# One head in eight: the softmax maxima added by an accumulating DMA in place of a GpSimd subtraction (LSH attention and gated feed-forward, one core)

## The chip, the cores and the metric

The kernel runs on one core of one Trainium2 chip. The metric is the device time of one launch in microseconds (us). The kernel before took 1372.26 us (median of 3 runs, 1371.28 to 1372.66).

## The reference

The input x is 16 sequences of 512 positions with 128 features, float32. Two residual blocks follow each other; the layer norms have no learned scale.

```
x = x + ln(attn(ln(x)))        # 16 heads of 8 features; queries also serve as keys
x = x + ln(ffn(ln(x)))

attn: q = x Wq^T + bq; v = x Wv^T + bv
      bucket(s,h) = 6 sign bits of [q, 1] . hyperplanes, read as a number of 0..63
      logits[s,t] = (q_s . q_t) / sqrt(128) * (62 + (bucket_s == bucket_t))
      out = softmax(logits) v
ffn:  h = silu(x w1^T s1) * (x w2^T s2); h = gelu(h h1^T s); h = gelu(h h2^T s); h w3^T s3
```

What matters here is the softmax. The matrix of logits of a head is symmetric (the coefficient is, and the keys are the queries), so the maximum of row s is also the maximum of column s. The kernel subtracts the maxima along columns, takes the exponential, and multiplies from the left with the values and a column of ones.

## The kernel before, in words

**Work.** 16 sequences of 16 heads make 256 heads, numbered j. A head's logits are a tile `l` of 128 partitions x 4 x 512 float32 (1 MB), of which there are 11 buffers (`LB`). Each head passes these steps:

- `gather` (L787): SP, the queue of the SyncE engine, issues three loads, `ql` and `qr` (72 rows of 512 bf16: the queries, split into three bf16 parts) and `bb` (the bucket numbers, the same row on all 128 partitions). Four heads can be loaded ahead.
- `scores` (L838): four TensorE (PE) matmuls `sp` into PSUM, three PSUM banks for them. `coeffs` (L855): VectorE (DVE) makes four tiles `co` of coefficients, 62 or 63, from `bb`.
- `logits` (L879): four DVE instructions multiply `co` with `sp` into `l` and leave the maximum of every row in one column of `mxpad`.
- `maxima` (L919): from head 4 on this is done for two heads together. DVE transposes `mxpad` in blocks into `mt` (128 x 32), and SP stores `mt` to DRAM as `md`, 16 KB.
- `softmax` (L933): SP loads a head's 512 maxima from `md` onto all 128 partitions (`mb`, 256 KB, three buffers); GpSimd (POOL) subtracts, `l = l - mb`, over 2048 elements a partition (L947); ScalarE (ACT) takes the exponential in place (L952).
- `attend` (L957): for each group of four heads, once all four exponentials are there, PE multiplies the values with them (`av`); ACT copies the result (`avs`), PE turns it back (`op`), DVE divides by the sums. Only then do the four `l` buffers come free.

`residual` (L1018) and `ffn` (L1041) follow per sequence. Their layer norms use POOL for one small power each (L450, 128 x 4), and the feed-forward uses PE (`w` L1088, `hp` L1122, `yp` L1156), ACT (silu L1074, gelu L1135) and DVE (`h` L1057). `inputs` (L510) prepares the input norms in three groups, with a power on POOL each (L561). Before the first feed-forward, PE fills its idle time with matmuls on zeros, `activity` (L1244).

**Order.** All steps are Python generators under a planner, the class `Order` (L47). It keeps a clock per engine; each step names its engine, a cost and a rank, and an engine that is free takes the ready step of lowest rank (ACT: the earliest, with a surcharge for a change of its function table). The order that results is written into each engine's instruction stream once and for all. On the chip every engine and each issuing queue works through its stream in that order; an instruction that waits holds up what is behind it. Three of the planner's lines matter:

```
            elif want[0] == "rest":
                self._at(self.now + want[1], self._step, p, None)
                return
```

A step `rest` makes a generator come back so many planned us later, and takes no engine; nothing of it is left in the instruction streams but the place of what follows.

Of the kernel before, what the change touches and what calls it, by code (L numbers as in the profile page):

```python
# [13 lines left out]
F32 = mybir.dt.float32  # L14
BF16 = mybir.dt.bfloat16
AF = mybir.ActivationFunctionType
ALU = mybir.AluOpType
# [4 lines left out]
P = 128  # L22
# [168 lines left out]
def tile_lsh_attention_ffn(  # L191
# [20 lines left out]
    nc = tc.nc  # L212
    B, S, E = x.shape
# [4 lines left out]
    NT = S // P  # L218
    NC = HID // P
    GH = 4  # L220
    NG = H // GH
    Q = P // GH
# [9 lines left out]
    SCALE = 1.0 / math.sqrt(E)  # L232
    AHEAD = 1
    MH = 2
    LB = 11
    SLOTS = H * NT
    N = B * SLOTS
# [3 lines left out]
    p2 = ctx.enter_context(tc.tile_pool(name="p2", bufs=2))  # L241
    ps_b = ctx.enter_context(tc.tile_pool(name="ps_b", bufs=1, space=PSUM))
    dram = ctx.enter_context(tc.tile_pool(name="dram", bufs=2, space=DRAM))

    od = Order()
# [17 lines left out]
        out=hb_sb,  # L263
        in_=hyper[DH].unsqueeze(0).unsqueeze(2).to_broadcast([H, NH, 1]),
# [73 lines left out]
    def dve(cost, rank, emit):  # L338
        return ("op", "DVE", cost, emit, rank, None)

    def act(cost, rank, emit, table=None):
        return ("op", "ACT", cost, emit, rank, table)

    def pool(cost, rank, emit):
        return ("op", "POOL", cost, emit, rank, None)

    def dma(kb, rank, emit, held=True, cost=0.35):
        return ("dma", "SP", cost, emit, rank, None, kb, held)

    def get(kind):  # L350
        return ("get", kind)
# [4 lines left out]
    def events(n):  # L356
        return [Event() for _ in range(n)]
# [4 lines left out]
    banks = Pool("b", 2)  # L362
    logit_bufs = Pool("l", LB)
    row_bufs = Pool("r", 4)
# [10 lines left out]
    gathered, exped = events(B * H), events(B * H)  # L375
# [503 lines left out]
    def logits():  # L879
        for j in range(B * H):  # L880
            kl = yield get(logit_bufs)
            if j < SINGLES or j % MH == 0:
                km, pair = (yield get(mx_bufs)), []
# [28 lines left out]
            pair.append((j, l))  # L912
            if j < SINGLES or len(pair) == MH:
                od.spawn(maxima(pair, mx, km))
# [4 lines left out]
    def maxima(heads, mx, km):  # L919


        mt = p2.tile([P, Q], F32, tag="mt", name=f"mt_{heads[0][0]}")
        yield dve(0.14, 0, lambda: nc.vector.transpose(mt, mx))
        od.put(mx_bufs, km)

        md = dram.tile([Q, GH, Q], F32, tag="md", name=f"md_{heads[0][0]}", bufs=4)
        yield dma(
            16, 0, lambda: nc.sync.dma_start(out=md.rearrange("t k q -> k t q"), in_=mt), cost=0.6
        )
        for i, (j, l) in enumerate(heads):  # L930
            od.spawn(softmax(j, l, md[i * NT : (i + 1) * NT]))

    def softmax(j, l, md):  # L933

        km = yield get(mb_bufs)
        mb = p1.tile([P, S], F32, tag=km, name=f"mb_{j}")
        yield dma(
            256,
            0,
            lambda: nc.sync.dma_start(  # L940
                out=mb, in_=md.rearrange("t k q -> (t k q)").partition_broadcast(P)
            ),
        )
        yield pool(
            4.52,
            1,
            lambda: nc.gpsimd.tensor_tensor(  # L947
                l, l, mb.unsqueeze(1).to_broadcast([P, NT, S]), op=ALU.subtract
            ),
        )  # L950
        od.put(mb_bufs, km)
        yield act(1.82, 0, lambda: nc.scalar.activation(l, l, AF.Exp, scale=SCALE), "exp")  # L952
        od.set(exped[j])
# [367 lines left out]
```

## Time and profile before

| | |
|---|---|
| time, median of 3 runs | 1372.26 us (1371.28 to 1372.66) |
| the profiled execution: its time / its span | 1373.08 us / 1371.3 us |
| granted TensorE clock, mean | 0.991 |
| first `w` matmul (the feed-forward begins) | 169.9 us |
| last logits instruction of DVE | 1263 us |
| last POOL subtraction ends | 1281.5 us |
| DMA, mean over the span | 128 GB/s |

The span runs from the first to the last instruction; 1.8 us of the execution's time lie around it. The kernel has a start of some 25 us until the first logits, a long middle in which attention of one sequence and feed-forward of earlier ones run together, and, from 1263 us, an end of 108 us in which the last two feed-forwards run alone. Shares of busy time over the whole span mix these three.

### The profile page before, as it was taken

The numbers are of one execution on the slowest core, as the hardware profiler recorded it, in microseconds if no ns is written. First come the engines' busy times: TensorE is split into PE (matmuls) and PEld (weight loads), VectorE is DVE, ScalarE is ACT, GpSimd is POOL, SyncE is SP. The second block draws the span as 40 slices with busy tenths as digits, with TensorE's granted clock in tenths as the row PEclk, the third lists the DMA queues.
The fourth block names the chain that finished last, engine by engine and source line by source line (L and its number), as shares of the span: only waits on it lengthen the run. The fifth ranks groups of instructions, "written<-read, shape, count | busy, mean of one in ns | idle before, by whom it ended". The sixth has DMA issues, their size and how long they took to land.

```text
span 1371.3 us, 21177 instructions
## 1 busy us (share of the span) xinstructions
PE 1317.3 (96%) x5922; PEld 550.9 (40%) x5922; DVE 1236.0 (90%) x3989; ACT 1127.8 (82%) x1607; POOL 1217.1 (89%) x319
## 2 busy tenths in 40 slices
PE   9999999999889999999999999999999999999996
PEld 3433334334334434343434434343434434343443
DVE  5999999999889999999999999999999999998210
ACT  2567798999779888988989888988989888988852
POOL 1599999999999999999999999999999999999400
PEclk9999999999899999999999999999999999999998
DMA  5756455445435455445545455454545454453000
GB/s 143 194 148 157 133 150 145 140 140 141 134 106 153 125 130 142 138 138 132 147 116 147 129 134 135 139 139 135 142 124 141 135 134 135 132 122 101 24 8 8
DMA packets 159837, 175.39 MB, mean 128 GB/s; under 512 B 34280, under 2 KB 117480, under 8 KB 159720
## 3 DMA queue, kind: packets, MB, share of 16 engines
q1 hardware_dynamic: 156909, 170.56, 45.4%
q10 hardware_dynamic: 2811, 3.48, 0.8%
q8 instruction: 47, 0.77, 0.2%
q14 instruction: 70, 0.57, 0.1%
HBM read 154.81 MB, written 19.17 MB: 127 GB/s over the span
## 4 chain that ended last, share of the span: by engine, by line
PE 50%; DVE 24%; POOL 9%; issue 8%; DMA 6%; ACT 2%; SPq 1%; POOLq 0%; DVEq 0%; ACTq 0%
PE hp L1122 18%; PE av L973 12%; DVE l L894 11%; PE sp L847 9%; DVE co L865 8%; POOL l L947 8%; PE w L1088 4%; PE yp L1156 3%; DMA mb<-md 3%; DMA bb<-bkd 1%; DMA qd<-q 1%; PE op L994 1%; PE vp L760 1%; POOL rs_x L561 1%; DMA qr<-qd 1%
## 5 line engine op out<-in xcount | busy, mean ns | idle before, releaser
L947 POOL TENSOR_TENSOR l<-l,mb 128x2048 f32<-128x2048 f32 x256 | 1156.1, 4552 | 43.4 <-DVE mxpad L894 24.0
L894 DVE CUSTOM_DVE_ANT_0 l<-co,sp 128x512 f32<-128x512 bf16 x1024 | 665.7, 681 | 13.8 <-PE av L973 6.9
L952 ACT ACTIVATE l<-l 128x2048 f32<-128x2048 f32 x256 | 484.6, 1907 | 40.9 <-POOL l L947 39.4
L1122 PE MATMUL hp<-h,h 128*128 128x512 f32 x1024 | 498.6, 596 | 0.3 <-ACT h L1135 0.3
L865 DVE TENSOR_SCALAR co<-bb,bj 128x516 bf16<-128x516 bf16 x1024 | 455.0, 472 | 3.3 <-DMA bb<-bkd 3.1
L847 PE MATMUL sp<-qr,ql 72*128 72x512 bf16 x1024 | 358.0, 382 | 26.7 <-DVE mxpad L894 22.5
L1122 PEld LDWEIGHTS hp<-h,h 128*128 128x128 f32 x1024 | 190.1, 190 | 185.6 <-issue 151.6
L973 PE MATMUL av<-l,vaug 128*32 128x512 f32 x2048 | 263.6, 603 | 0.0
L847 PEld LDWEIGHTS <-ql 72*128 72x128 bf16 x1024 | 94.1, 97 | 313.9 <-issue 290.7
L1088 PE MATMUL w<-xnt_f,w 128*128 128x512 f32 x256 | 132.0, 601 | 2.5 <-ACT a L1074 2.4
L952 ACT ACT_TABLE_LOAD x86 | 110.3, 1283 | 1.5
L1251 PE MATMUL activity<-still 128*128 128x512 bf16 x402 | 106.6, 385 | 1.0 <-DVE still L280 1.0
L973 PEld LDWEIGHTS av<-l,vaug 128*32 128x32 f32 x2048 | 47.4, 109 | 116.5 <-issue 93.9
L894 DVE DVE_READ_ACCUMULATOR2_ANT mxpad<- 128x1 f32 x1024 | 85.7, 84 | 0.0
L450 POOL TENSOR_TENSOR rs_y<-ve_y,mhalf 128x4 f32<-128x4 f32 x16 | 16.1, 1006 | 67.1 <-issue 34.7
L1057 DVE TENSOR_TENSOR h<-w,a 128x512 f32<-128x512 f32 x64 | 43.7, 682 | 35.2 <-PE w L1088 30.3
L1135 ACT ACT_TABLE_LOAD x58 | 74.4, 1283 | 0.9
L987 ACT COPY avs<-av 128x512 f32<-128x512 f32 x64 | 37.0, 578 | 40.0 <-PE av L973 39.9
L1088 PEld LDWEIGHTS w<-xnt_f,w 128*128 128x128 f32 x256 | 46.9, 191 | 53.1 <-issue 21.8
L1156 PEld LDWEIGHTS yp<-w,h 128*128 128x128 f32 x512 | 65.0, 196 | 7.3 <-issue 4.0
L1156 PE MATMUL yp<-w,h 128*128 128x128 f32 x512 | 66.6, 281 | 0.1
L1251 PEld LDWEIGHTS <-still 128*128 128x128 bf16 x402 | 39.1, 99 | 56.5 <-issue 19.0
(94 smaller groups left out, 941.7 us busy)
## 6 DMA issues: line engine op xcount, KB each, us to landing
mb<-md SPq DMA_DIRECT2D x256, 256.0 KB
bb<-bkd SPq DMA_DIRECT2D x256, 130.5 KB
ql<-qd SPq DMA_DIRECT2D x256, 72.0 KB
qr<-qd SPq DMA_DIRECT2D x255, 72.0 KB
qd<-q SPq DMA_DIRECT2D x96, 128.0 KB
xta<-in_L_attn_x_dram SPq DMA_DIRECT2D x16, 256.0 KB
xtr<-in_L_attn_x_dram SPq DMA_DIRECT2D x16, 256.0 KB
out_dram<-y SPq DMA_DIRECT2D x16, 256.0 KB
```

The lines of the kernel that those rows point to most:

```text
L847: nc.tensor.matmul(sp, lhsT=ql[:, ts(t, P)], rhs=qr, start=True, stop=True)
L865: nc.vector.tensor_scalar(co, bb.rearrange("p (r c) -> p r c", c=BP)[:, :, 0:BC], bjs[b][:, c : c + 1], float(NBKT - 2), op0=ALU.is_equal, ...
L894: nc.vector.tensor_tensor_reduce(out=l, in0=co[:, 0:S], in1=sp, scale=1.0, scalar=-3.0e38, op0=ALU.mult, op1=ALU.max, accum_out=mx[:, t : ...
L947: lambda: nc.gpsimd.tensor_tensor(l, l, mb.unsqueeze(1).to_broadcast([P, NT, S]), op=ALU.subtract),
L952: yield act(1.82, 0, lambda: nc.scalar.activation(l, l, AF.Exp, scale=SCALE), "exp")
L973: nc.tensor.matmul(av[k * Q : (k + 1) * Q, :], lhsT=va[:, t, c : c + Q], rhs=ls[gg * GH + k][0][:, t, :], start=(t == 0), stop=(t == NT - 1),)
L1057: lambda: nc.vector.tensor_tensor(h[:, c, :], g2, a, op=ALU.mult),
L1088: lambda: nc.tensor.matmul(gp, lhsT=w_sb[which][:, 0, ts(c, P)], rhs=xnt, start=True, stop=True),
L1122: lambda i=i: nc.tensor.matmul(hp, lhsT=w[:, i, ts(c, P)], rhs=hin[:, i, :], start=(i == 0), stop=(i == NC - 1),),
L1135: nc.scalar.activation(h[:, c, :], hp, AF.Gelu, scale=sc[:, c : c + 1])
L1156: nc.tensor.matmul(yp[:, ts(t, E)], lhsT=h[:, i, ts(t, P)], rhs=w_sb["w3"][:, i, :], start=(i == 0), stop=(i == NC - 1),)
L1251: nc.tensor.matmul(bk, lhsT=still, rhs=still.unsqueeze(1).to_broadcast([P, NT, P]), start=start, stop=stop,)
```

## The change

In each group of eight heads the one with j mod 8 = 4, 32 of the 256, takes another way (`negated`). It is always the first of a pair of `maxima`. ACT writes the negated maxima of the pair, `mn` (128 x 32), SP stores them to DRAM as `mdn`, and POOL issues one DMA that adds the head's 512 negated maxima onto all 128 x 4 rows of `l` (1 MB). After a planned rest of 12 us, ACT takes the exponential. For these heads the load of `mb` and the POOL subtraction are gone. The store of `md` stays, for the second head of the pair.

```diff
+    EVERY = 8
...
+        by_dma = [j % EVERY == EVERY // 2 for j, _ in heads]
+        if any(by_dma):
+            mn = p2.tile([P, Q], F32, tag="mn", name=f"mn_{heads[0][0]}")
+            mdn = dram.tile([Q, GH, Q], F32, tag="mdn", name=f"mdn_{heads[0][0]}", bufs=2)
+            od.spawn(negated(heads[0], mt, mn, mdn))
         for i, (j, l) in enumerate(heads):
-            od.spawn(softmax(j, l, md[i * NT : (i + 1) * NT]))
+            if not by_dma[i]:
+                od.spawn(softmax(j, l, md[i * NT : (i + 1) * NT]))
+
+    def negated(head, mt, mn, mdn):
+        j, l = head
+        yield act(0.25, -2, lambda: nc.scalar.activation(mn, mt, AF.Copy, scale=-1.0))
+        yield dma(
+            16,
+            0,
+            lambda: nc.sync.dma_start(out=mdn.rearrange("t k q -> k t q"), in_=mn),
+            cost=0.6,
+        )
+        row = mdn[0:NT].rearrange("t k q -> (t k q)").partition_broadcast(P)
+        yield pool(
+            1.3,
+            0,
+            lambda: nc.gpsimd.dma_start(
+                out=l,
+                in_=row.unsqueeze(1).to_broadcast([P, NT, S]),
+                accum_op=ALU.add,
+            ),
+        )
+        yield ("rest", 12.0)
+        yield act(1.82, 0, lambda: nc.scalar.activation(l, l, AF.Exp, scale=SCALE), "exp")
+        od.set(exped[j])
```

Since the planner orders all steps anew, every engine's stream changes. Counted in the two built programs, POOL's stream has 224 subtractions and 32 DMAs in place of 256 subtractions; SP's has 32 loads fewer and 32 stores more; ACT's has 32 instructions more; the first `w` matmul of the feed-forward stands behind 113 score matmuls instead of 126, and `activity` has 364 matmuls instead of 402. Behind the last score matmul PE has the same work left but for one `hp` matmul more.

## The prediction

> **What bounds the kernel now.** I read the page's first part, then the busy time by stretches, since the shares of the whole span mix start, middle and end.
>
> ```profile
> PE 1317.3 (96%) x5922; PEld 550.9 (40%) x5922; DVE 1236.0 (90%) x3989; ACT 1127.8 (82%) x1607; POOL 1217.1 (89%) x319
> ```
>
> Three engines look nearly full. The stretches (columns: stretch, its length, then busy us of PE, PE's weight loads, DVE, ACT, POOL, the clock, DMA share and GB/s) tell them apart:
>
> ```profile
> 100.00:400.00 300.00, 281.03 (x1300) 112.82 (x1299) 286.50 (x924) 258.07 (x422) 293.74 (x73) 0.98 0.51 140
> 400.00:1263.00 863.00, 845.15 (x3838) 352.43 (x3838) 854.78 (x2758) 759.37 (x948) 844.18 (x214) 1.00 0.49 134
> 1263.00:1371.30 108.30, 95.17 (x345) 46.81 (x343) 14.72 (x55) 61.80 (x118) 23.52 (x10) 0.97 0.04 15
> ```
>
> From 400 to 1263 us DVE is busy 99.0% of the time, POOL 97.8%; before 400 POOL is the fuller one (97.9% against 95.5%). The last 108 us are PE's, with DVE and POOL nearly idle. So the middle can shorten by DVE's idle time at most: 13.5 us from 100 to 400, 8.2 us after. What DVE waits for there is in the waits, sorted by engine (us in total, times, longest):
>
> ```profile
> DVE l L894 <- PE av L973: 6.9, 6, 2.3
> DVE l L894 <- PE sp L847: 5.1, 17, 1.1
> DVE nm_f L455 <- POOL rs_f L450: 3.8, 3, 2.8
> DVE nm_x L571 <- POOL rs_x L561: 3.4, 2, 2.9
> DVE nm_o L455 <- POOL rs_o L450: 2.3, 1, 2.3
> ```
>
> The first is DVE without a free `l` buffer: `av` gives them back, after POOL and ACT. The last three are small POOL instructions that stand behind subtractions.
>
> The groups give the prices:
>
> ```profile
> L947 POOL TENSOR_TENSOR l<-l,mb 128x2048 f32<-128x2048 f32 x256 | 1156.1, 4552 | 43.4 <-DVE mxpad L894 24.0
> L952 ACT ACTIVATE l<-l 128x2048 f32<-128x2048 f32 x256 | 484.6, 1907 | 40.9 <-POOL l L947 39.4
> ```
>
> **What goes.** 32 subtractions. Back to back they follow each other at 4.51 us (seven end to end took 31.58 us, in POOL's timeline just before its backlog ends), so POOL loses 32 x 4.51 = 144 us of 1217. 32 loads of `mb` go too: 8.4 MB of 175 MB, and 32 x 0.38 us of SP's issuing.
>
> Little of the 144 us reaches the end, because DVE stands beside POOL with as much work. In the chain of waits the same eight `hp` matmuls of a sequence begin at 453.88 and, six sequences on, at 918.40: 77.4 us per sequence, 38.7 us per eight heads. POOL spends 8 x 4.51 + 1.9 (its 1 us powers and `rs_x`, 60 us spread over 256 heads) = 38.0 of these; DVE 99%, 38.3. With the change POOL has 33.5 us plus the issue of one DMA, and DVE still 38.3.
>
> Does DVE itself run faster beside an idler POOL? No: two `co` in a row take 0.87 us both at 28.6 us, before POOL's first subtraction, and at 614.7 us beside one; over the whole run `co` lies within 430 to 488 ns.
>
> So what can come back is the part of DVE's waits that POOL causes: 6.9 + 3.8 + 2.3 = 13.0 us. (The 2.9 us of `nm_x` is the 6.8 us of the `rs_x` power itself and stays.) I take half, 6.5 us: `av` waits for PE and ACT as well. The same bound holds early on, where POOL is behind; the feed-forward starts 13 score matmuls sooner, but DVE's work until 1263 us does not shrink for it.
>
> At the end POOL works off a backlog: seven subtractions without a gap from 1249.9 to 1281.5 us, then the exponential of head 255 at 1286.5, and the `av` of the last group ends at 1292.5. With head 252 on the DMA the last subtraction is bounded by its own data: SP issues the last `mb` loads from 1265.5 to 1268.3 us, they land 3.3 to 4.1 us later (the DMA pieces of the chain), and two subtractions make 1281; if the first of the two is loaded early enough to run under that, 1278. ACT's new order also puts that exponential ahead of a pair of silus. PE's remaining work is unchanged. I take 3 us.
>
> **What comes, and what hides it.**
>
> - ACT: 32 small instructions. The nearest row, a 128x4 ACTIVATE (`ve_f`, 295 ns), makes 9.6 us. ACT is busy 44.0 of 50 us in the middle (759 of 863), which leaves 4.6 us per eight heads; it hides there. Without that cover it costs up to 9.6 us.
> - SP: 32 stores of 16 KB, priced as `md` (0.56 us each, 18 us), for 12 us of `mb` issues that go. SP issues some 2.6 us a head (0.78 + 0.72 + 0.43 + 0.38 and half of 0.56) of 4.84. A new wait stands in its queue: the store waits for ACT's negation, and `ql`, `qr`, `bb` and `md` stand behind. An ACT that is one exponential and a table change late (1.9 + 1.3 us) delays them by 3 us; four heads are loaded ahead, some 14 us, which covers it.
> - POOL: the DMA waits for its store to land, with the next subtraction behind it. The store is the size of `md`, whose landing SP waited for at most 1.4 us beyond plan, in all 7.0 us; POOL's own new slack (below) is larger.
> - The issue on POOL: no row of this trace shows a DMA issued there. Low end: SP's shortest issue, 0.32 us. High end: POOL's slowest row per element, the power of 128x40 in 6.76 us, 0.17 us per element; with 512 rows in 16 queues, 32 each, 5.4 us. I take four times SP's `mb` issue (four times the rows): 1.5 us. POOL then needs 35.0 of 38.7. Up to an issue of 5.2 us it stays under 38.7.
>
> The Trainium skill speaks against the edit here ("SBUF — State Buffer", Who interferes with whom, and its box on DVE blocking DMA): descriptors of a GpSimd DMA are written through ports that a two-port DVE instruction locks, and it tells of a 620 ns DMA stretched to 3100. Stretched likewise, an estimate from that page, 1.5 us would be 7.5 and POOL's excess 32 x 2.3 = 74 us. In this trace the subtractions, which use POOL's ports throughout, lie within 4512 and 4630 ns beside a DVE that is 99% busy, so no lock is seen; of descriptors no run here shows anything.
>
> - The transfer. Nothing here adds to memory by DMA, so from both sides, by this row (packets, MB, share of the 16 engines):
>
> ```profile
> q1 hardware_dynamic: 156909, 170.56, 45.4%
> ```
>
> 170.56 MB in 45.4% of 16 x 1371.3 us is 17.1 KB per us and engine, so 1 MB on 16 engines takes 3.8 us. Low end: that, plus the fixed part of an `mb` landing (3.3 to 4.1 us less 1.0 for its 256 KB, so 2.4 to 3.1): 6.2 us. High end: each row read twice, 7.7 us, on engines that are 45% taken, 14 us, plus 3.1: 17 us. I take 11: twice the data, idle engines, fixed part.
>
> Who waits for it is ACT, whose exponential stands in line with gelus and copies behind it. Its place in the new ACT stream is after the exponential of the head two further on, or later (31 of 32). That head's maxima come 9.7 us after this pair's (two heads of 4.84); `md`, `mb` and its subtraction take some 7 + 4.5 us more, its exponential 1.9: 23 us after the pair's maxima. The DMA goes out some 5 us after them (negation, store, landing). So about 18 us are covered, more than the high end. I cost the transfer at nothing.
>
> The sum: 6.5 + 3 = 9.5 us back, less 3 us for waits that a new order brings at random: 6.5 us off the profiled execution's 1373.08, 1366.6; against the median, 0.8 us lower, **1366 us**.
>
> **Rivals.**
>
> 1. *Nothing.* DVE at 99% and PE at the end keep the time, and the half I took comes back as other waits: 1372, within 0.2% (2.7 us, about what a measurement here can tell from no change). For it: 17 short waits for `sp` that have nothing to do with POOL.
> 2. *The landing becomes ACT's wait (slower).* If the DMA takes more than 18 us, ACT stands at its exponential 32 times, with silu, gelu and `avs` queued behind it, for whose banks PE waits. ACT's 4.6 us of idle time take up part; I count half. At 20 us: 32 x 2 / 2 = 32 us, 1404; at 24 us 96 us. For it: nothing prices an add inside a DMA. Against it: my high end already counts two reads and full contention.
> 3. *POOL's issue costs more than 5.2 us.* Then POOL is the bound: at 6.5 us, 32 x 1.3 = 42 us, 1414. Against it: my high end is 5.4.
> 4. *It doesn't do what it says*, since the planner orders all anew: the two streams differ from the first instructions on. The granted clock fell to half for 10 us near 365 us; if that moves or doubles, 5 us either way. This widens 1 and the forecast, and has no case of its own.
>
> **Numbers.** Forecast 0.50 (1355 to 1369.5: the low end gives back all 13.0 us of DVE's waits and 5 us at the end), nothing 0.15, rival 2 0.23, rival 3 0.12. Faster 0.50, same 0.15, slower 0.35. The range runs from 1355 to 1410: below it lie 0.03, above it half of rival 3 and a third of rival 2, 0.14.
>
> **What would show it.** DVE busy over 99% from 100 to 1263 us, with its waits for `av` and the powers down by half; POOL some 90% in the middle; the last logits near 1257 us. Wrong would be: ACT waiting at L961 for a DMA by more than a us each; a POOL DMA over 5 us between two subtractions; DVE below 98% with waits for `bb` (SP held up by the new store).

## The result and the profile after

| | before | after |
|---|---|---|
| time, median of 4 runs each | 1371.77 us | 1421.54 us (1415.58 to 1426.33) |
| ratio, 95% interval | | 1.036 (1.0313 to 1.0408) |
| the profiled execution: time / span | 1373.08 / 1371.3 us | 1415.58 / 1413.8 us |
| granted TensorE clock, mean | 0.991 | 0.975 |
| first `w` matmul | 169.9 us | 158.0 us |
| last logits instruction of DVE starts | 1262.5 us | 1297.0 us |
| last `av` matmul ends | 1292.5 us | 1329.5 us |

The kernel is 3.6% slower, 50 us, where a gain of 6 was forecast. I read the profile after in the order of the prediction. First the page: busy time by engine, the queues (packets, MB, share of the 16 engines), and the accumulation's row among the DMA issues (KB each, median us from issue to landing).

```profile
PE 1330.6 (94%) x5884; PEld 549.8 (39%) x5884; DVE 1237.5 (88%) x3989; ACT 1131.5 (80%) x1640; POOL 1116.7 (79%) x319
...
q1 hardware_dynamic: 156525, 162.69, 41.3%
q0 software_dynamic: 16896, 33.56, 14.5%
...
l<-mdn POOLq DMA_DIRECT2D x32, 1024.0 KB, 11.6
```

POOL has lost 100 us of busy time, as the change meant (144 us of subtractions less 32 issues of 1.30 us). DVE, ACT and PE have what they had before, so nobody works longer (PE's 13 us more, with 38 `activity` matmuls fewer, fit the lower clock). The new queue q0 takes 14.5% of the 16 engines: 0.145 x 1413.8 / 32 = 6.4 us of all 16 for one accumulation. Then the stretches after, in the columns of the prediction:

```profile
100.00:400.00 300.00, 277.25 (x1257) 109.23 (x1255) 276.30 (x888) 246.38 (x402) 254.27 (x70) 0.96 0.62 154
400.00:1300.00 900.00, 865.41 (x3865) 356.97 (x3864) 869.30 (x2806) 776.45 (x1002) 794.27 (x219) 0.98 0.61 151
1300.00:1414.00 114.00, 95.14 (x342) 46.56 (x340) 14.40 (x52) 60.03 (x117) 16.64 (x8) 0.93 0.09 22
```

From 400 us on DVE is busy 96.6%, not 99.0%; before 400 us 92.1%, not 95.5%. Its idle time from 100 to 1300 us, about the end of the logits, is 54 us; from 100 to 1263 it was 21.7. POOL stands at 88%. No engine is the bound of the middle any more, and the time is longer: something makes all of them wait in turn. The waits of DVE from 100 to 1260 us name it in part (us in total, times, longest):

```profile
DVE l L895 <- PE sp L848: 11.1, 20, 2.9
DVE co L866 <- DMA bb<-bkd: 8.4, 6, 2.9
DVE h L1088 <- PE w L1119: 6.2, 13, 1.2
DVE l L895 <- PE av L1004: 5.6, 5, 2.7
DVE rd L1035 <- PE op L1025: 4.7, 13, 1.2
DVE nm_f L456 <- POOL rs_f L451: 4.7, 3, 2.8
```

The second line is new in this stretch: four heads are loaded ahead, and still the row of bucket numbers comes late. In the whole run POOL waits for `mb` far more than before (14.1 us then):

```profile
L978 POOL TENSOR_TENSOR l<-l,mb 128x2048 f32<-128x2048 f32 x224 | 1018.3, 4584 | 174.5 <-DMA mb<-md 136.4
```

How that looks in one place, in POOL's timeline (start, length, instruction, and in brackets the idle time before it with what ended it):

```profile
177.53 9.04 POOL L978 TENSOR_TENSOR l<-l,mb 128x2048 f32<-128x2048 f32 x2
186.51 1.31 POOL L954 DMA_DIRECT2D l<-mdn  x1
199.12 8.99 POOL L978 TENSOR_TENSOR l<-l,mb 128x2048 f32<-128x2048 f32 x2 [11.30 <-DMA mb<-md]
```

and in SP's timeline beside it:

```profile
188.13 0.78 SPq L799 DMA_DIRECT2D ql<-qd  x1
189.02 1.16 SPq L971 DMA_DIRECT2D mb<-md  x2
```

POOL issues the accumulation at 186.51. SP issues the next `mb` at 189.02, 2.5 us later. POOL can use it at 199.12: 10.1 us for a load whose landing the prediction read as 3.3 to 4.1 us. It runs beside the 1 MB on the same 16 engines. How busy these are meanwhile, in the columns of the stretches:

```profile
192.51:198.51 6.00, 6.00 (x32) 2.84 (x29) 5.96 (x20) 1.98 (x4) 0.00 (x0) 1.00 1.08 199
```

The DMA share is 0.61 from 400 to 1300 us, but 1.08 here: the engines are full. The trace also lists every packet that the engines moved, with its start and length. By that list an accumulation lasts 8.5 us from its first packet to its last (median of 32); of the 16 engines' time in that while its packets take 75% and the loads' 25%, where the loads have 45.4% over the whole of before. The loads' packets are no longer than before (those of 2 KB: 106 ns on average, against 108). So the loads come late because they stand in line, not because each packet is slow.

### The profile page after: what moved, and what is told of

Same layout as the page of the kernel before. It is cut to its first block, busy times and chain, and to the rows that moved or that the text cites. A ratio compares the mean times of both kernels' runs of the same rounds, so it can differ in the third digit from the quotient of the medians.

```text
span 1413.8 us, 21096 instructions
## 1 busy us (share of the span) xinstructions
PE 1330.6 (94%) x5884; PEld 549.8 (39%) x5884; DVE 1237.5 (88%) x3989; ACT 1131.5 (80%) x1640; POOL 1116.7 (79%) x319
## 3 DMA queue, kind: packets, MB, share of 16 engines
q0 software_dynamic: 16896, 33.56, 14.5%
## 5 line engine op out<-in xcount | busy, mean ns | idle before, releaser
L978 POOL TENSOR_TENSOR l<-l,mb 128x2048 f32<-128x2048 f32 x224 | 1018.3, 4584 | 174.5 <-DMA mb<-md 136.4
L983 ACT ACTIVATE l<-l 128x2048 f32<-128x2048 f32 x224 | 426.8, 1908 | 51.6 <-POOL l L978 50.5
L866 DVE TENSOR_SCALAR co<-bb,bj 128x516 bf16<-128x516 bf16 x1024 | 449.8, 471 | 13.2 <-DMA bb<-bkd 13.0
L1004 PE MATMUL av<-l,vaug 128*32 128x512 f32 x2048 | 273.4, 615 | 6.5 <-ACT l L961 5.6
L1119 PE MATMUL w<-xnt_f,w 128*128 128x512 f32 x256 | 136.0, 616 | 7.7 <-ACT h L1166 7.6
L1282 PE MATMUL activity<-still 128*128 128x512 bf16 x364 | 97.6, 387 | 1.0 <-DVE still L281 1.0
L1187 PEld LDWEIGHTS yp<-w,h 128*128 128x128 f32 x512 | 68.1, 201 | 17.3 <-issue 11.4
L1187 PE MATMUL yp<-w,h 128*128 128x128 f32 x512 | 69.5, 284 | 0.6 <-ACT h L1166 0.4
L1166 ACT ACTIVATE h<-hp,h2s 128x512 f32<-128x512 f32 x64 | 41.6, 685 | 32.7 <-PE hp L1153 32.3
## 6 DMA issues: line engine op xcount, KB each, us to landing
l<-mdn POOLq DMA_DIRECT2D x32, 1024.0 KB, 11.6
```

Of the source, the lines that this page charges most:

```text
L866: nc.vector.tensor_scalar(co, bb.rearrange("p (r c) -> p r c", c=BP)[:, :, 0:BC], bjs[b][:, c : c + 1], float(NBKT - 2), op0=ALU.is_equal, ...
L978: lambda: nc.gpsimd.tensor_tensor(l, l, mb.unsqueeze(1).to_broadcast([P, NT, S]), op=ALU.subtract),
L1004: nc.tensor.matmul(av[k * Q : (k + 1) * Q, :], lhsT=va[:, t, c : c + Q], rhs=ls[gg * GH + k][0][:, t, :], start=(t == 0), stop=(t == NT - 1),)
L1119: lambda: nc.tensor.matmul(gp, lhsT=w_sb[which][:, 0, ts(c, P)], rhs=xnt, start=True, stop=True),
L1166: nc.scalar.activation(h[:, c, :], hp, AF.Gelu, scale=sc[:, c : c + 1])
L1187: nc.tensor.matmul(yp[:, ts(t, E)], lhsT=h[:, i, ts(t, P)], rhs=w_sb["w3"][:, i, :], start=(i == 0), stop=(i == NC - 1),)
```

## The experiments

All times are medians; each stands against runs of the kernel before on the same chip (1372.6 to 1374.1 us). A run that leaves maxima out of the subtraction, or puts wrong ones in, scales the exponentials concerned by 0.001 so that they stay finite; its diff below leaves that line out.

**Is it the bytes, the add, or the new order?**

`g_after_noacc`: all of the change but the transfer itself.

```diff
         yield pool(1.3, 0,
-            lambda: nc.gpsimd.dma_start(out=l, in_=..., accum_op=ALU.add),
+            lambda: None,
         )
```

> After with the accumulating DMA not issued at all; negation, store and the order stay, and the exponentials of these 32 heads are scaled by 0.001 over logits without their maxima subtracted, so the output is not the reference's. Theory O (the new order by itself costs some us): 1374 to 1378, as with the 32 KB transfers (1377). Theory P (the order is free, and POOL's relief pays once nothing is transferred): 1366 to 1370.

Measured: 1376.19 us against 1372.59, ratio 1.0038 (1.0025 to 1.0052). The new order with POOL's relief costs 3.6 us; without any transfer there is still no gain.

`e1_small`: the same DMA, but 32 KB.

```diff
-                out=l,
-                in_=row.unsqueeze(1).to_broadcast([P, NT, S]),
+                out=l[:, 0, 0:64],
+                in_=row[:, 0:64],
```

> The kernel after, in exactly its order, but each of the 32 accumulating DMAs covers 128 x 64 elements (32 KB) instead of 128 x 2048 (1 MB); the rest of the subtraction is left out for these heads (their exponential is scaled down so that it stays finite). Theory A, the late store: the 1 MB transfer holds the DMA engines, the small md store behind it lands up to 7 us late, SP stands at the mb load with the gathers behind. Then the loss goes with the bytes: 1360 to 1372 us, SP waiting for md under 15 us in all (129 in the kernel after), granted clock back to 0.985 or more. Theory B, the order: the new streams, with one more store that waits for ACT in SP's queue, lose the time whatever the DMA moves: 1405 to 1425 us, and SP still waits for md.

Measured: 1377.17 us, ratio 1.0034 (1.0019 to 1.0049), 5 us above the first range expected and 28 below the second. So 32 DMAs on POOL, with their stores, negations and waits, cost no more than the order. Nearly all of the loss needs the bytes.

`e2_plain`: 1 MB copied, not added (`accum_op` left out).

> The kernel after in the same order, but the 32 DMAs copy the 1 MB onto l instead of adding it (the logits of these heads are lost; their exponential is scaled down). The bytes read from DRAM and written are the same; the read of the old l and the add are gone. Theory A with the add as the price: a 2 KB packet falls from 200 ns towards the 106 ns of the mb loads, the transfer from 8.5 to about 5 us, the loss to about half: 1385 to 1400 us. If the bytes alone count, 1412 to 1425 us. Theory B, the order: 1405 to 1425 us.

Measured: 1424.64 us, ratio 1.0372 (1.0339 to 1.0406), the same as after. The add is not the cause.

`e5_quarter` and `e4_every16` change the dose: 256 KB in each of 32 heads (`out=l[:, 0, :], in_=row`), and 1 MB in 16 heads (`EVERY = 16`).

> After with only the first 512 of the 2048 elements of a partition accumulated, 256 KB in place of 1 MB, as much as one load of mb, in the same order; the exponentials of these heads are scaled by 0.001 over logits with three quarters not subtracted, so the output is not the reference's. If the loss goes in proportion to the bytes: 1377 + 45 / 4 = 1388. If what hurts is the length of one hold of the engines beyond what the prefetched loads cover: below 1380, near the order's own 1376.

> One head in sixteen instead of one in eight: 16 accumulating DMAs. Theory A: half of the occurrences, about half of the loss: 1390 to 1402 us, SP's wait for md about 65 us. Theory B: the loss is one of order and need not go with the number: anywhere from 1372 to 1425 us.

Measured: 1380.50 us, 1.0049 (1.0032 to 1.0067), and 1406.60 us, 1.0250 (1.0217 to 1.0282), both a little above the ranges expected. Taken from the order's 1376 (the order with 16 heads was not timed alone), 8 MB in quarters cost 4 us (the intervals hardly tell that from nothing), 17 MB in whole pieces 30 us and 34 MB 45 us. The loss is not in proportion to the bytes: the small pieces are nearly free. That fits a lead of the loads that covers a short hold of the engines and not a long one; it doesn't show it. The traces fit it too: a quarter lasts 3.1 us from its first packet to its last, and from 4 to 9 us after its issue the engines' share is 0.58 on average, where in after it is 1.05.

**Do the bytes alone do it, in the old order?** `e6_extra` leaves before as it is and sends 32 plain copies of 1 MB within DRAM from ACT's queue, for which nothing waits.

```diff
+        def issue():
+            nc.sync.dma_start(out=md.rearrange("t k q -> k t q"), in_=mt)
+            if heads[0][0] % 8 == 4:
+                nc.scalar.dma_start(out=spare, in_=...)
...
```

> The kernel before, in its own order and with all its subtractions, plus 32 plain transfers of 1 MB (DRAM to DRAM, rows of 2 KB) that nothing waits for, issued from ACT's queue where the maxima of heads 4, 12, 20, ... are stored. Theory A (the bytes on the DMA engines delay the small md store and the loads around it): 1400 to 1425 us, and SP waits for md by 60 us or more in all (7 before). Theory B (what is left of order, POOL queue and the new exponential's place makes the bytes costly only in the new stream): under 1385 us.

Measured: 1462.19 us, ratio 1.0652 (1.0629 to 1.0675): 89 us, more than either range expected. No step of the computation changed its place, and nothing waits for the copies. What they add are ACT's 32 issues (0.55 us each, 18 us on an engine that is busy 77%) and the hold on the DMA engines; the first alone can't make 89 us. DVE's waits show the second (3.1 and 2.3 us in before):

```profile
DVE co L866 <- DMA bb<-bkd: 30.6, 19, 7.5
DVE nm_o L456 <- POOL rs_o L451: 24.7, 9, 4.3
```

Why it costs more than the 45 us of after is not shown. POOL, 97.8% busy in the middle of before, has no slack for a late `mb` here (it waits 76.9 us for it, 14.1 in before), and the second line may come from that; a copy also lasts a little longer than an accumulation (9.4 us from its first packet to its last).

**Is it SP, held at `md`?** In after SP waits 129.2 us for the store of `md` to land before it issues `mb` (before: 7.0), with later heads' loads behind it in its queue:

```profile
SPq L971 <- DMA md<-mt: 129.2, 48, 7.7
```

`e8_after_const` and `e9_before_const` let every `mb` load read a constant DRAM row, which needs no wait.

```diff
+    nc.sync.dma_start(out=mdc.rearrange("t k q -> k t q"), in_=mxpads[0])
...
-                out=mb, in_=md.rearrange("t k q -> (t k q)").partition_broadcast(P)
+                out=mb, in_=mdc[0:NT].rearrange("t k q -> (t k q)").partition_broadcast(P)
```

> The kernel after in its order, but every mb load reads a constant row of DRAM that was stored once at the start, so that SP never waits for md to land; the md stores are still made, and the accumulating DMA is whole. The true maxima are left out of the subtraction (the exponential is scaled down to stay finite). Theory A with SP's stand at md as the channel: most of the 49 us comes back, 1370 to 1385 us. Theory C, the loads themselves (bb, ql, qr, mb) are slowed by sharing the engines: the loss stays, 1405 to 1425 us, with DVE waiting for bb and POOL for mb.

> The same edit on the kernel before: every mb load reads a constant row, SP never waits for md. SP waited for md by 7 us in all there, so under every theory little is won: 1366 to 1373 us. It is the base line for the run on the kernel after.

Measured: 1417.81 us, 1.0327 (1.0311 to 1.0343), and 1373.37 us, 1.0004 (0.9995 to 1.0013). SP's wait ahead of `mb` was gone and 44 of the 50 us stayed, so the theory that SP's stand at `md` is the channel of the loss falls. The loads, issued in time, still came late, by the waits of `e8_after_const`:

```profile
POOL l L980 <- DMA mb<-mdc: 106.9, 38, 7.6
DVE co L868 <- DMA bb<-bkd: 19.3, 14, 3.2
```

**Which loads?** Three cuts, each made in after and in before, with the planner's order kept: the row loads `ql`, `qr`, `bb` only for the first four heads; no load of `mb` (zeros are subtracted); neither.

```diff
-            lambda: nc.sync.dma_start(out=bb, in_=bkds[b][h].partition_broadcast(P)),
+            lambda: j == j0 and nc.sync.dma_start(out=bb, in_=...),
...
-        mb = p1.tile([P, S], F32, tag=km, name=f"mb_{j}")
+        mb = mbc
```

> After, with the loads of ql, qr and bb left out for all but the first four heads: later heads compute from those four heads' rows, so the output is not the reference's. The planner still counts the loads, so every other instruction keeps its place. mb loads and the 32 accumulations stay. Theory G (late gathers are the channel: DVE waits for bb, PE for ql and qr, and PE's gaps cost clock): the time falls to the nogather version of before, within 8 us, some 1372 to 1380. Theory M (late mb loads are the channel: POOL waits 136 us for them): most of the loss stays, 1405 or more, less what a shorter DMA queue gives mb. Theory Q (any load behind the 1 MB is late because bytes stand ahead of it; taking out half the other bytes does not help the ones left): between, about half the loss.

> Before with the same loads of ql, qr and bb left out, as the baseline: 1365 to 1373 by every theory, since before waits for these loads 4.3 us in all.

> After without any load of mb: POOL subtracts a constant tile of zeros, and the exponentials are scaled by 0.001 to stay finite, so the output is not the reference's. Everything else keeps its place. Theory M: the time falls to the version of before without mb loads, within 8 us, or below it. Theory G: DVE still waits for bb (8 us or more from 100 to 1300 us) and PE still comes late, 1400 or more. Theory Q: about half the loss goes.

> Before without any load of mb, as the baseline: 1360 to 1373 by every theory, since POOL waits for mb only 5 us in the middle, and the end saves some 3 us of landing.

> After with both left out: the loads of ql, qr and bb for all but the first four heads, and every load of mb (a constant tile of zeros is subtracted, the exponentials are scaled by 0.001), so the output is not the reference's. The 32 accumulations of 1 MB and the order stay. Theory Q (the transfer costs only by what the loads beside it lose): within 6 us of the same cut of before, some 1365 to 1374. Theory W (the transfer also costs by itself, as by writes into the memory that DVE and ACT use, or by late stores): the 14 us that were left with one kind of load gone stay, 1378 or more.

> Before with the same loads left out, as the baseline: 1363 to 1368 by both theories (each cut alone gave 1368).

| left out | before, us | after, us | after less before |
|---|---|---|---|
| nothing | 1371.8 | 1421.5 | 50 |
| row loads | 1367.9 | 1384.6 | 17 |
| `mb` loads | 1368.4 | 1382.6 | 14 |
| both | 1369.4 | 1377.6 | 8 |

The ratios to the kernel before are 1.0077 (1.0048 to 1.0105) and 0.9960 (0.9945 to 0.9975) without row loads; 1.0062 (1.0044 to 1.0080) and 0.9965 (0.9953 to 0.9978) without `mb`; 1.0028 (1.0011 to 1.0044) and 0.9973 (0.9958 to 0.9988) without both. The last pair stands 0.55% apart, which its intervals don't tell from the order's 0.38%; 1377.6 us lies between the two ranges expected, which left the order's cost out. So the 34 MB are nearly free once these loads no longer run beside them, though the engines are nearly as full behind a piece as in after (0.99 from 4 to 9 us after its issue): that the transfer costs by itself has no support. Taking away either kind of load returns some two thirds. So neither "DVE waits for `bb`" nor "POOL waits for `mb`" is the channel alone; these expectations, and the one of half each, missed. Each cut also shortens the queue for the other kind (POOL's wait for `mb` is 52.1 us without the row loads, 136.4 with them). How the loss divides between late rows and late maxima can therefore not be read from these runs.

POOL's waits alone mislead here: in `g_after_noacc` POOL also waits 91.0 us for `mb`, at 1376 us. It has become early, and waits where it used to work. DVE's waits carry the greater part of the difference. Here they are for `g_after_noacc`, from 100 to 1260 us:

```profile
DVE l L895 <- PE sp L848: 7.9, 17, 1.9
DVE l L895 <- PE av L1000: 6.0, 5, 2.7
DVE rd L1031 <- PE op L1021: 5.0, 13, 1.2
DVE h L1084 <- PE w L1115: 4.1, 12, 0.8
DVE vaug L769 <- PE vp L761: 0.3, 1, 0.3
```

All the waits that this view has for DVE in this stretch sum to 23.3 us, in after to 45.9. What came in between is `bb` (8.4), POOL's small powers (8.3 against nothing, probably since POOL, held up by `mb`, is late for them too) and a later PE (`sp` and `w`, 5.3). That is 22.6 of the 32 us by which the last logits come later than in `g_after_noacc`. Of the rest, 3.5 us arise before 100 us and 3 after 1260, and DVE's own work up to there is 2.7 us longer.

**Would a plan that knows of the transfer be better?** `e3_planned` tells the planner that the DMA engines are taken for 8.5 us; `e7_split` sends four quarters with planned rests of 3.4 us between them.

```diff
+        od.queue = max(od.queue, od.now) + 8.5
```

```diff
+        for t in range(NT):
+            yield pool(1.1, 0, lambda t=t: nc.gpsimd.dma_start(out=l[:, t, :], ..., accum_op=ALU.add))
+            if t < NT - 1:
+                yield ("rest", 3.4)
+        yield ("rest", 6.0)
```

> The kernel after, but the planner counts each accumulating DMA into its DMA queue (8.5 us, the median from its first to its last packet), so that mb loads and what depends on them stand later in the streams. Theory A: SP no longer stands at mb loads (129 us falls under 50) and the gathers go ahead; half of the loss or more comes back: 1370 to 1395 us. Theory B: another order, another time, with no side foretold: 1400 to 1430 us.

> The kernel after, but each accumulation is issued as four DMAs of 256 KB, one per 512 columns, with 3.4 us of planned rest between them, so that the same bytes come in four short bursts. If the length of a burst counts (a store that comes into it waits for its rest, up to 7 us): md at most 2 to 3 us late, SP's wait for md under 70 us (129), 1385 to 1405 us. If the total of the bytes counts: 1410 to 1430 us. POOL issues 96 DMAs more, at 1.3 us each at most 125 us, which its new idle time takes.

Measured: 1496.56 us, 1.0905 (1.0883 to 1.0926), and 1470.55 us, 1.0714 (1.0696 to 1.0732). Both are far slower than after, and than every range expected. DVE's largest wait in `e3_planned` points to the reason:

```profile
DVE l L895 <- PE av L1005: 80.8, 34, 6.3
```

In `e7_split` the same wait is 54.5 us; in after it is 5.6. It is DVE without a free `l` buffer: a head that stays longer in flight keeps its buffer, and DVE runs out of the 11. The increase, 75 and 49 us, is about what the two lose against after (75 and 49). Hiding a transfer by more time takes buffers that this kernel doesn't have.

**What was POOL's relief worth?** `g_before_nosub` keeps the old order and leaves out 32 subtractions and their `mb` loads.

```diff
+        left_out = j % 8 == 4
...
-            lambda: nc.gpsimd.tensor_tensor(
+            lambda: left_out or nc.gpsimd.tensor_tensor(
```

> Before in its own order with 32 of the 256 mb loads and subtractions (heads 4, 12, 20 and so on) left out; their exponentials are scaled by 0.001, so the output is not the reference's. It measures POOL's relief alone. As the prediction had it (half of DVE's 13 us of waits and 3 us at the end): 1361 to 1367. If DVE and PE hold the middle whatever POOL does: 1369 to 1373.

Measured: 1372.50 us against 1372.59, ratio 0.9997 (0.9983 to 1.0010): nothing. Its stretches, in the columns of the prediction:

```profile
100.00:400.00 300.00, 284.56 (x1302) 112.76 (x1300) 285.86 (x920) 255.67 (x420) 252.00 (x63) 0.97 0.46 133
400.00:1263.00 863.00, 842.95 (x3838) 350.52 (x3836) 853.89 (x2757) 757.99 (x947) 748.95 (x193) 1.00 0.46 127
```

POOL falls from 97.8 to 86.8% in the middle, and DVE stays at 98.9%. `f_last` puts the accumulation on head 252 alone (`by_dma = [j == 252 ...]`).

> After with the accumulation for head 252 alone, every other head subtracted on POOL as before; the reference's output. The prediction's term for the end: 3 us back, 1369 to 1370. From the run without 32 subtractions, which returned nothing: 1372 to 1377, a new order's few us and no gain.

Measured: 1378.60 us, ratio 1.0042 (1.0029 to 1.0056). One accumulation, with the order that it brings, costs as much as 32 small ones. The loss lies at the end: in the profiled execution the last logits come 1.8 us sooner than in before, but from there to the end of the span it takes 113.8 us, not 108.8. The last `mb` loads are issued at 1263.65, 1.75 us after the accumulation, and POOL can use the first at 1273.29, 9.6 us later. No version that I ran and that computes the whole beats before.

## Why the prediction was wrong, point by point

1. **The transfer: the step that failed.** The prediction said: "Who waits for it is ACT", found 18 us of cover against a landing of 6.2 to 17, and "I cost the transfer at nothing". Every part of that was right for the landing: it took 11.6 us (9.9 to 14.2; taken: 11), and ACT waited for it twice, 1.5 us in all. But it asked only who waits for this transfer, not who waits behind it. One accumulation takes 6.4 us of all 16 engines, and the loads of the next heads go through the same ones. The term was zero; the runs give it 1421.5 - 1376.2 = 45 us, which the runs without loads trace to loads that come late. The row was in view: the prediction quoted q1's 45.4% and used it to stretch the accumulation by the loads, and not the loads by the accumulation. A mean share of some 60% (0.61 from 400 to 1300 us in after) looks like room and isn't: behind an accumulation the engines are full.

   A row of the Trainium skill bears on this, and I had not weighed it: "DMA: Bandwidth & Descriptors" (SWDGE vs HWDGE vs iDMA) says that DMAs issued by GpSimd and those of the other engines feed different queues inside each of the same engines, and that the engine takes turns between them. The late `mb` above (10.1 us, on engines that are full) agrees with it as far as sharing goes; that the turns are even, no run here shows.

2. **The gain: 6.5 us from DVE's waits and 3 us at the end; measured nothing.** The bound by DVE was right: POOL 11 points idler left DVE at 98.9%. Half of DVE's 13 us was wrong, in two ways. The lines added up to 13.0 us were those of the whole span; from 100 to 1260 us before has 5.7 us for `av` and 1.0 for `nm_f`, and the rest lies in the start and the end. And the waits did not fall with POOL relieved: over the whole of `g_before_nosub` the three are 11.8 + 3.0 + 2.3 = 17.1 us. So POOL was not what the wait for `av` hung on; whether PE or ACT was, no run separates. The end was wrong because the step took POOL's backlog for the bound there. In `g_before_nosub` the last subtraction ends at 1279.4 us, 2 us sooner, and the last exponential starts at 1287.7, not 1286.5: between the two ACT has three table loads, the exponential before, a pair of silus and two small activations. `f_last`, with the changed order, is 5 us longer there, by its last `mb`.

3. **Three us for a new order: right in size, by luck.** 3.6 us by `g_after_noacc`, with POOL's relief in it; the prediction names no row that its 3 us come from.

4. **In after the end lost 8 us.** From the last logits to the end of the span: 116.8 us, in `g_after_noacc` 1373.8 - 1265.2 = 108.6. POOL's timeline shows it:

```profile
1296.74 1.31 POOL L954 DMA_DIRECT2D l<-mdn  x1
1297.61 5.02 POOL L978 TENSOR_TENSOR l<-l,mb 128x2048 f32<-128x2048 f32 x1
1310.40 8.97 POOL L978 TENSOR_TENSOR l<-l,mb 128x2048 f32<-128x2048 f32 x2 [7.78 <-DMA mb<-md]
```

   In SP's timeline beside it stand the last store of `md` and the last two `mb` loads:

```profile
1298.00 0.53 SPq L929 DMA_DIRECT2D md<-mt  x1
1306.39 0.80 SPq L971 DMA_DIRECT2D mb<-md  x2
```

   The accumulation of head 252 goes out 1.3 us ahead of this store, and SP waits 7.7 us for the store to land before it issues the loads (in `g_after_noacc` they follow the same store 2.0 us after its issue). The loads then take the usual 4.0 us to 1310.40. The step wanted two subtractions "loaded early enough"; their maxima stood behind that very transfer, and POOL stood 7.8 us. Here SP's stand at `md` is the channel, 16 KB behind 1 MB; in `f_last` the store was on time and the load was late instead. The other 32 of the 40 us between the two profiled executions lie ahead of the last logits (1297.0 against 1265.2).

5. **The issue on POOL: right.** 1.30 us (1.20 to 1.47), taken 1.5, break-even 5.2. The negation on ACT took 227 ns (taken 295; 32 of them are 9.4 us, not 9.6), and PE and POOL waited 3.5 us for it in all; SP's stores took 0.57 us each.

6. **The rivals.** None was it. "Nothing" is right for the gain (`g_before_nosub`) and wrong for the time. The second, ACT waiting for the landing, had the right object and the wrong victim. The third's condition did not arise: an issue of 1.30 us is far from 5.2.

7. **What was to show it.** Of the signs of a wrong prediction one came true: "DVE below 98% with waits for `bb` (SP held up by the new store)". DVE's share is 96.6% from 400 us on, and `bb` stands in its waits. The bracket is not the cause: in `g_after_noacc` the stores stay and DVE has no wait for `bb` in the middle. Of the signs of being right only POOL's came, 88% where some 90% was said; the last logits came at 1297 us, not near 1257.

**What stays open.** PE's granted clock fell with the rest: (1 - 0.975) x 1413.8 = 35 us of clock lost, 19 in `g_after_noacc`, 12 before. Whether PE's gaps caused by late loads cost the clock, or the clock in turn delays the loads' consumers, no run separates. That quarters were nearly free because the engines are not full for long fits the traces of `e5_quarter`, but no run has the full bytes in quarters: `e7_split`, meant for that, ran out of `l` buffers.

## What to carry to other kernels

Ask of a new transfer not only who waits for it but which loads stand beside it on the same engines, how long one piece holds them, and how far ahead those loads are issued; a mean DMA share of 60% is no answer to that, since the share beside one piece can be full. Before moving work off an engine that stands beside a full one, leave that work out and time it: here that one run would have told that POOL's 144 us were worth nothing. Where waits grow on an engine that was just relieved, compare with a run in which the relief costs nothing (`g_after_noacc`) before calling them a loss.

## What the runs showed of the hardware beyond that

- A 1 MB transfer issued by POOL, from a row broadcast to all partitions, took 6.4 us of the 16 engines as an add and 0.129 x 1423.0 / 32 = 5.7 us as a copy; the prediction had worked out 3.8 for 1 MB from the loads' rows. With the other loads gone (`n_after_neither`) the add still took 9.8 us from issue to landing, so most of the 11.6 is its own.
- Its issue on POOL took 1.30 us for 1 MB and 0.90 us for 256 KB and for 32 KB, beside a DVE that was busy 97% of the time. The stretch from 620 to 3100 ns that the prediction cited from "SBUF — State Buffer" shows in none of the 32 issues (1.20 to 1.47 us) and landings (9.9 to 14.2 us); whether a DVE instruction of this kernel locks the ports that the page speaks of, no run shows.
- The loss from holding the DMA engines was steep in the size of a piece: some 4 us for 32 pieces of 256 KB (3.1 us from the first packet to the last), 45 us for 32 of 1 MB (8.5 us).
- A store of 16 KB can stand behind such a piece as a load can: SP waited up to 7.7 us for `md` in after, at most 1.4 us in before.
